# Writing the keys' copy ahead of the values' products over the upper dims, in a four-layer perceiver kernel

## The chip, the cores and the metric

The kernel runs on one core of one Trainium2 chip. The metric is the device time of one execution in microseconds. Before the change the median of 3 runs is 3023.78 us (3019.76 to 3024.86).

## What is computed

A stream `x` of 128 tokens by 256 dims passes four layers. Each layer has a cross-attention over one context of 12544 tokens by 192 dims, an attention among the 128 tokens, and a layer of experts. All of it is float32. What the change touches is the cross-attention of layers 0, 1 and 2, which is in all three of this kind (layer 0 without biases and with a mask over the context, layers 1 and 2 with biases, layer 1 with scores clipped to 10000):

```
q = (layernorm(x) @ Wq + bq)   split in 16 heads of 16
k = (context @ Wk + bk)        split in 16 heads of 16
v = (context @ Wv + bv)        split in 16 heads of 16
out = softmax(q k^T / 4) v
x = x + out @ Wo + bo
```

Layer 3's cross-attention has heads of 64 and code of its own (`KeysInTurn`, `attend_once`).

## The kernel before

**Blocks and groups.** The context is cut in 25 blocks of 512 tokens (`NSB`, `SB`; the last has 256). The 16 heads are two groups `g` of eight, 128 of the 256 dims each. For each group the keys and values of all blocks are made in SBUF, a first sweep over the blocks finds each query's highest score, and a second sweep over chunks of 128 tokens makes exponentials and sums. So a layer has two first sweeps, each of which also projects the keys and values that it will need.

**The context's dims.** A block's context arrives transposed, in two tiles. `ctxA` has the lower 128 dims for 512 tokens. `ctxB` has the upper 64 dims: the first 256 tokens on partitions 0 to 63, the other 256 on partitions 64 to 127. A product over all 192 dims is therefore made in two steps: over `ctxA` (`low` = 0) and, added in PSUM, over `ctxB` (`low` = 1). `halves(b)` lists the two halves of 256 tokens.

**One block's projection** (`project`, L153). The keys and the values of a block share one PSUM tile `p` of 128 partitions by 2 x 512 floats, a "pair". Half `i` holds the keys of its 256 tokens in columns 0 to 255 and the values in columns 256 to 511. `project` is called twice a block. With `low` = 0 it takes a new pair and writes the keys' products over `ctxA` (`keys_into`, L105: two products of 128 x 256) and the values' (`values_into`, L117: four of 128 x 128). With `low` = 1 it adds the same over `ctxB`. Then `keep_keys` (L128) copies the keys to SBUF and `keep_values` (L135) the values; both are one ScalarE instruction (L131 a copy, L133 the same with a bias, L137 a copy). All products are issued by the helper `mm`, L103, so their line is always L103.

**Where blocks are projected.** Each layer projects 44 blocks with values in this way: 8 (layers 1 and 2) or 2 (layer 0) ahead of the attention (`early`, in tiles `kv`, into one PSUM pair of a pool of its own), two between the first group's second sweep and the second group's first (L794), and the rest within the first sweeps. For the last three blocks of a sweep only the keys are made so; their values follow later (`project_values`). Those early blocks and the two between sweeps are placed by the framework's scheduler.

**The order in a first sweep.** `steps` (L139) spreads the blocks to be projected over the 25 steps, two blocks ahead of their use. Within a step `in_order` (L225) keeps TensorE, VectorE and ScalarE to the written order: first the projection, then the scores of the step.

- Masked (layer 0): `highest` is called twice a step. It makes the scores of one block for 8 x 128 queries in two pairs (L558 adds the mask, L559 is the score), and VectorE takes their maxima (L565). Four maxima a step.
- Unmasked (layers 1 and 2): `over` makes scores of the difference of two blocks' keys (L559; the difference is made by GpSimd in `apart`, L570) and ScalarE applies Relu (L578, two a step); `highest_of_two` makes the scores of the other block and VectorE adds them and takes the maximum (L586, four a step).

**PSUM.** In a first sweep the pool `ppr` has four pairs, taken in turn. A step that projects takes five: one for the projection and four for scores. So the last scores of a step take the pair that the projection has just left, and the next projection takes the pair of the step's first scores.

Of the kernel before, what the change touches and what calls it, by code (L numbers as in the profile page):

```python
# [28 lines left out]
HB = SB // 2  # L29
NSB = -(-S2 // SB)  # L30
# [23 lines left out]
class Keys:  # L54
# [98 lines left out]
    def project(self, g, b, low, values=True):  # L153


        if g * NSB + b < self.done:
            return
        if not low:
            self.add_up(g, b)
            self.started[g, b] = self.net.early_pair() if self.rest is None else self.net.pair()  # L160
        p = self.started[g, b]
        self.keys_into(p, g, low, [b])
        if values:
            self.values_into(p, g, low, [b], HB)
        if low:
            n = len(self.halves(b))
            self.keep_keys(g, b, p[:, :n, :HB])
            if values:
                self.keep_values(g, b, p[:, :n, HB:])
            self.done = g * NSB + b + 1  # L170

    def project_values(self, g, blocks):
        p = self.net.pair()
# [1737 lines left out]
```

## Time and profile before

| | |
|---|---|
| median of 3 runs | 3023.78 us |
| the profiled execution | 3021.48 us, span 3019.8 us |
| mean granted TensorE clock | 0.975 |
| L103 into `pair`, keys over ctxA | 1236 products, 399 ns each in the mean |
| L131, keys' copy without bias, 128 x 512 | 586 ns median, 48 + 2 times |
| L133, keys' copy with bias, 128 x 512 | 687 ns median, 100 times |
| L137, values' copy | 579 ns median, 150 times |
| L565, maximum, layer 0 | 1215 ns median |
| L578, Relu, layers 1 and 2 | 1024 ns median |

The first sweeps lie at about 20 to 160 and 280 to 415 us (layer 0), 660 to 760 and 910 to 1030 (layer 1), 1310 to 1430 and 1555 to 1690 (layer 2).

PE is TensorE's products, PEld its loads of the stationary operand, DVE VectorE, ACT ScalarE, POOL GpSimd, SP the queue that issues most DMAs. A line of the timeline gives start, duration, engine, line of the kernel, operation, tile written and tiles read, and how many instructions were merged (`x8`). A float32 product appears as two records. The bracket at the end tells how long the engine was idle before and whose end released it. Ends of products are modelled by the profiler.

### The profile page before, as it was taken

Reading aid. Unit: us, or ns where it says so; the run is one execution under the profiler, and the core shown is the slowest. Engines: PE = TensorE matmul, PEld = TensorE weight load, DVE = VectorE, ACT = ScalarE, POOL = GpSimd, SP = SyncE. Lnnn points to the kernel's source line nnn. Section 1 sums busy time; section 2 is a strip of 40 time slices with the busy share of each in tenths; the row PEclk is TensorE's granted clock in tenths of the full one; section 3 lists DMA queues with packets and bytes.
Section 4 is the critical chain, followed back from the end, with each engine's and each line's share of the span. In section 5 each row is a group of like instructions: output and inputs, shape, how many; then the busy total and the mean of one; then the engine's idle time right before and its main releaser. Section 6 shows DMA issues by size and latency. Waiting matters only on the chain.

```text
span 3019.8 us, 79794 instructions
## 1 busy us (share of the span) xinstructions
PE 2882.8 (95%) x34893; PEld 2209.0 (73%) x34893; DVE 2024.2 (67%) x3241; ACT 1626.2 (54%) x1904; POOL 282.7 (9%) x504
## 2 busy tenths in 40 slices
PE   8999999989999999999999998899999999999969
PEld 5677667455676576765776675688989989889858
DVE  6876887525893598745544555577777777777844
ACT  1176148335685585245875682355655656555521
POOL 7011021223001100211001002000000000000000
PEclk9999999999999999999999998999999999999979
DMA  5201210562002202521012007232322223222436
GB/s 133 61 19 32 72 39 6 189 225 57 21 3 79 59 4 88 175 82 53 15 39 73 23 3 258 92 98 80 85 84 83 85 79 88 85 78 83 136 111 201
DMA packets 177706, 247.28 MB, mean 82 GB/s; under 512 B 32459, under 2 KB 119269, under 8 KB 177358
## 3 DMA queue, kind: packets, MB, share of 16 engines
q1 hardware_dynamic: 165592, 227.26, 24.8%
q0 software_dynamic: 11008, 14.37, 1.6%
q8 instruction: 274, 4.49, 0.6%
q10 hardware_dynamic: 758, 0.55, 0.1%
q14 instruction: 74, 0.61, 0.1%
HBM read 241.56 MB, written 0.13 MB: 80 GB/s over the span
## 4 chain that ended last, share of the span: by engine, by line
PE 83%; DVE 11%; ACT 2%; DMA 1%; issue 1%; SPq 1%; POOL 0%; ACTq 0%; DVEq 0%; POOLq 0%
PE pair L103 21%; PE acc L699 10%; PE pair L559 8%; PE v L103 8%; PE sc L859 6%; PE pair L629 5%; PE acc L901 5%; PE ps L279 5%; PE one L629 4%; DVE parts L565 3%; PE pair L622 2%; PE acc L279 2%; PE kv L103 2%; PE ps L1698 1%; DVE over L586 1%
## 5 line engine op out<-in xcount | busy, mean ns | idle before, releaser
L586 DVE CUSTOM_DVE_ANT_0 over<-over,pair 128x512 f32<-128x512 f32 x384 | 241.2, 683 | 249.2 <-PE pair L559 237.6
L103 PE MATMUL pair<-ctxA,wk 128*128 128x256 f32 x1236 | 328.7, 399 | 6.5 <-ACT over L578 1.8
L103 PEld LDWEIGHTS pair<-ctxA,wk 128*128 128x128 f32 x1236 | 217.0, 190 | 138.5 <-ACT over L578 53.0
L861 ACT COPY kept<-sc 128x1024 f32<-128x1024 f32 (+1 forms) x135 | 136.2, 1009 | 261.2 <-PE sc L859 261.2
L565 DVE TENSOR_REDUCE parts<-pair 128x2 f32<-128x1024 f32 (+1 forms) x216 | 235.7, 1157 | 41.8 <-PE pair L559 41.8
L290 DVE TENSOR_TENSOR top<-top,kept 128x1024 f32<-128x1024 f32 (+2 forms) x145 | 169.1, 1169 | 134.0 <-ACT kept L861 132.7
L293 DVE SCALAR_TENSOR_TENSOR e<-pair,floor 128x1024 f32<-128x1024 f32 x196 | 227.3, 1217 | 14.6 <-PE pair L629 14.6
L677 ACT ACTIVATE e<-pair 128x1024 f32<-128x1024 f32 x196 | 200.7, 1025 | 46.5 <-PE pair L629 26.0
L654 ACT ACTIVATE e<-e 128x1024 f32<-128x1024 f32 x196 | 206.7, 1057 | 35.3 <-DVE e L293 24.3
L629 PE MATMUL pair<-qz,kT 32*128 32x256 f32 x2112 | 218.9, 374 | 0.0
L699 PE MATMUL acc<-e,v 128*17 128x128 f32 x6336 | 211.4, 274 | 3.0 <-ACT e L692 2.2
L699 PEld LDWEIGHTS acc<-e,v 128*17 128x17 f32 x6336 | 155.8, 97 | 67.8 <-ACT e L692 45.6
L692 ACT ACTIVATE e<-e 128x1024 f32<-128x1024 f32 x196 | 205.0, 1048 | 0.0
L293 DVE SCALAR_TENSOR_TENSOR e<-one,maskcol,less 128x256 f32<-128x256 f32 x392 | 162.6, 477 | 53.3 <-PE one L629 43.3
L859 PE MATMUL sc<-qz,kT 64*128 64x128 f32 x2816 | 197.8, 279 | 0.0
L559 PE MATMUL pair<-kT,qz 32*128 32x512 f32 (+1 forms) x1120 | 192.7, 592 | 5.2 <-DVE parts L586 3.8
L578 ACT ACTIVATE over<-pair 128x1024 f32<-128x1024 f32 x192 | 186.9, 1021 | 14.7 <-PE pair L559 7.4
L103 PEld LDWEIGHTS v<-wv,ctxA 128*128 128x128 f32 x1568 | 189.8, 192 | 6.4 <-issue 1.7
L103 PE MATMUL v<-wv,ctxA 128*128 128x128 f32 x1568 | 193.1, 276 | 0.0
L103 PE MATMUL pair<-ctxB,wk 64*128 64x256 f32 x1236 | 188.9, 399 | 0.0
L290 DVE TENSOR_TENSOR e<-one,less 128x512 f32<-128x512 f32 x196 | 126.3, 686 | 88.6 <-PE pair L629 88.1
L859 PEld LDWEIGHTS sc<-qz,kT 64*128 64x128 f32 x2816 | 171.6, 187 | 13.0 <-issue 1.3
(457 smaller groups left out, 5637.7 us busy)
## 6 DMA issues: line engine op xcount, KB each, us to landing
ctxA<-in_ctxA SPq DMA_DIRECT2D x324, 256.0 KB
ctxB<-in_ctxB SPq DMA_DIRECT2D x339, 128.0 KB
w<-in_L_ffn_W SPq DMA_DIRECT2D x32, 1024.0 KB
ctxA<-in_ctxA POOLq DMA_DIRECT2D x36, 256.0 KB, 3.2
w<-in_L_ffn_w_gateT SPq DMA_DIRECT2D x8, 1024.0 KB
wu<-in_L_ffn_w_upT SPq DMA_DIRECT2D x8, 1024.0 KB
w<-in_L_ffn_w_downT SPq DMA_DIRECT2D x8, 1024.0 KB
w<-in_L_ffn_w1T SPq DMA_DIRECT2D x8, 1024.0 KB
```

Of the source, the lines that this page charges most:

```text
L103: self.nc.tensor.matmul(out, a, b, start=start and not low, stop=low == 1, skip_group_check=True)
L279: self.nc.tensor.matmul(out, lhsT, rhs, start=(i == 0), stop=(i == n - 1))
L290: self.nc.vector.tensor_tensor(out, a, b, op)
L293: self.nc.vector.scalar_tensor_tensor(out, a, s, b, op0, op1, **kw)
L559: nc.tensor.matmul(x, qz[r, g, s, :], k[r, :n], start=not by_mask, stop=True)
L565: nc.vector.tensor_reduce(parts[:, s, 2 * half : 2 * half + 2, i], x, AX.X, ALU.max)
L586: nc.vector.tensor_tensor_reduce(es[half][:, j, :], es[half][:, j, :], x[:, j, :], 1.0, -LARGEST, ALU.add, ALU.max, parts[:, s, 2 * half + ...
L629: nc.tensor.matmul(at, keys.kT(c // 4)[tiles[t], k], q, start=start, stop=True, skip_group_check=True)
L654: nc.scalar.activation(to, to, AF.Exp)
L692: nc.scalar.activation(to, to, AF.Exp)
L699: nc.tensor.matmul(acc[32 * t : 32 * t + 17, half, :], v[:, c % 4 + j, 4 * half + t, :], es[half][:, t // 2, j, t % 2, :], start=c + j + h ...
L859: nc.tensor.matmul(x[:, t, c : c + P], kT[r, c : c + P], qz[r, g, :], start=True, stop=True)
```

## The change

In the half with `low` = 1, `keep_keys` now stands between the keys' and the values' products; before it stood behind both. With `low` = 0 nothing differs. `keep_values` and the counter `done` keep their place at the end.

```diff
-        p = self.started[g, b]
+        p, n = self.started[g, b], len(self.halves(b))
+        if not low:
+            self.keys_into(p, g, low, [b])
+            if values:
+                self.values_into(p, g, low, [b], HB)
+            return
         self.keys_into(p, g, low, [b])
+        self.keep_keys(g, b, p[:, :n, :HB])
         if values:
             self.values_into(p, g, low, [b], HB)
-        if low:
-            n = len(self.halves(b))
-            self.keep_keys(g, b, p[:, :n, :HB])
-            if values:
-                self.keep_values(g, b, p[:, :n, HB:])
-            self.done = g * NSB + b + 1
+            self.keep_values(g, b, p[:, :n, HB:])
+        self.done = g * NSB + b + 1
```

## The prediction

> **What bounds the kernel now.** I read the page's engine line first, then the waits, then the timeline of one block in each kind of sweep, because a mean over 3020 us hides which wait ends last in the stage that is changed.
>
> ```profile
> PE 2882.8 (95%) x34893; PEld 2209.0 (73%) x34893; DVE 2024.2 (67%) x3241; ACT 1626.2 (54%) x1904; POOL 282.7 (9%) x504
> PE 83%; DVE 11%; ACT 2%; DMA 1%; issue 1%; SPq 1%; POOL 0%; ACTq 0%; DVEq 0%; POOLq 0%
> ```
>
> TensorE is busy for 95% of the span and makes 83% of the chain that ended last. What stops it inside a block is paid in full, unless it waits a little later anyway. So one block has to be followed. This is a block of layer 0 (the masked kind, four L565 maxima on VectorE):
>
> ```profile
> 77.12 0.73 PEld L103 LDWEIGHTS pair<-ctxA,wk 128*128 128x128 f32 x4 [0.92 <-DVE parts L565]
> 79.08 0.70 PE L103 MATMUL pair<-ctxB,wk 64*128 64x256 f32 x4
> 79.40 0.63 PEld L103 LDWEIGHTS pair<-wv,ctxB 64*128 64x128 f32 x8
> 79.61 0.61 PE L103 MATMUL pair<-wv,ctxB 64*128 64x128 f32 x8
> ...
> 80.27 0.59 ACT L131 COPY kT<-pair 128x512 f32<-128x512 f32 x1 [4.54 <-PE pair L103]
> 80.75 0.59 ACT L137 COPY v<-pair 128x512 f32<-128x512 f32 x1
> ...
> 81.46 4.62 DVE L565 TENSOR_REDUCE parts<-pair 128x2 f32<-128x1024 f32 x4 [1.00 <-PE pair L559]
> 82.74 0.73 PEld L103 LDWEIGHTS pair<-ctxA,wk 128*128 128x128 f32 x4 [0.92 <-DVE parts L565]
> ```
>
> The columns are start, duration, engine, line; the bracket is the idle time before and what ended it. The period is 82.74 - 77.12 = 5.62 us, and it is one closed loop with no slack: 3.03 us of projection on TensorE (77.12 to 80.15, where the next tiles' loads begin), 1.31 us until the first scores are ready (81.46), 1.215 us of the first maximum (median of L565) and a hand-over, whereupon the next projection gets its PSUM pair. The keys' last product ends at 79.08 + 0.70 = 79.78, the values' last at 79.61 + 0.61 = 80.22. The keys' copy starts at 80.27: 0.05 us behind the values, 0.49 us behind the keys.
>
> The same in layer 1 (layer 2 is alike), where the keys' copy adds a bias (L133) and ScalarE also makes the Relu of L578:
>
> ```profile
> 685.06 0.70 PE L103 MATMUL pair<-ctxB,wk 64*128 64x256 f32 x4
> 685.39 0.63 PEld L103 LDWEIGHTS pair<-wv,ctxB 64*128 64x128 f32 x8
> ...
> 686.14 0.31 PEld L559 LDWEIGHTS pair<-apart,qz 32*128 32x128 f32 x8
> 686.26 0.69 ACT L133 ACTIVATE kT<-pair,bk 128x512 f32<-128x512 f32 x1 [2.37 <-PE pair L103]
> 686.84 0.58 ACT L137 COPY v<-pair 128x512 f32<-128x512 f32 x1
> 687.36 1.94 ACT L578 ACTIVATE over<-pair 128x1024 f32<-128x1024 f32 x2
> 688.53 0.73 PEld L103 LDWEIGHTS pair<-ctxA,wk 128*128 128x128 f32 x4 [0.76 <-ACT over L578]
> ```
>
> The period is 688.53 - 683.11 = 5.42 us. Here the two copies stand on ScalarE ahead of the Relu whose end lets the next projection start, so this kind could gain from an earlier copy of the keys. Whether it does is shown by a block that makes keys alone, with no values' copy:
>
> ```profile
> 1020.44 0.31 PEld L559 LDWEIGHTS pair<-apart,qz 32*128 32x128 f32 x8 [0.33 <-issue]
> 1021.67 1.94 ACT L578 ACTIVATE over<-pair 128x1024 f32<-128x1024 f32 x2 [0.42 <-PE pair L559]
> 1022.74 0.73 PEld L103 LDWEIGHTS pair<-ctxA,wk 128*128 128x128 f32 x4 [1.13 <-ACT over L578]
> ```
>
> There ScalarE stands idle for 0.42 us and the Relu still starts 1.23 us behind the load of its products (1020.44), against 1.22 in the full block (686.14 to 687.36). The Relu waits for its products, not for the copies.
>
> **The change, part by part.** *What moves.* In the second half of a block (`low` = 1), one ScalarE instruction moves ahead of four TensorE products. No instruction is added or removed, and no DMA is issued in the moved lines. SP's load into a ctxB buffer waits for the values' products that read it (L397, 80.26), so it comes later by the stall, but it fills the buffer for a block four later, over 20 us. GpSimd's difference of two keys (L570, 1.27 us from 963.53) waits for a block's copies and is needed behind the next projection (964.55 + 3.03), 2.8 us of slack.
>
> *What it adds.* In the built program of the changed kernel the first of the four values' products over the upper dims has a new wait on ScalarE in 131 of 132 blocks, and the values' copy a wait of its own on TensorE. The keys' copy reads columns 0 to 255 of each half of the pair, the products write columns 256 to 511 of the same half; the program orders them as if they overlapped. Before, the order was products, copy; now it is copy, products. TensorE works in order, so behind the waiting product stand the other three, the eight score products of this block, and the next block; VectorE's first maximum (or ScalarE's Relu) waits for those.
>
> *The stall, masked block.* Keys' last product ends at 79.78; +0.05 hand-over as now; +0.586 for the copy (median of L131); +0.05 back to TensorE (the values' copy of 12.24 to 12.83 releases a TensorE load at 12.88) = 80.47, where the values' loads began at 79.40. **1.07 us per block.** A restart costs no more: a projection's keys take 0.76 from the first load to the next tile's both after a wait (77.12 to 77.88) and without one (275.63 to 276.39). Nothing behind gets shorter: the loop from the end of the projection to the next (scores, maximum) does not touch the copies. The two rows that bound this unknown: if the loads go ahead and only the product waits, its start moves from 79.61 to 80.47, 0.86; if the load of 0.21 (79.40 to 79.61) is not hidden at the restart, 1.28. I take 1.07, as every wait of L103 in the timeline holds the load too.
>
> *The stall, biased block.* 685.76 + 0.05 + 0.687 (median of L133) + 0.05 = 686.55 against 685.39: 1.16. ScalarE is free by then: it has been idle since 683.89. One thing comes back: the second copy now ends 0.58 earlier relative to the projection's end, and the last pair of scores, which waits for it, too. In the keys-only block the next projection starts 1022.74 - 1020.44 = 2.30 behind the score loads, in the full block 2.39. So 0.09 is won, since the Relu holds the rest. **1.07 per block**, bounds 0.95 - 0.09 = 0.86 and 1.37.
>
> *How many.* By the values' copies: L137 runs 102 + 30 + 18 = 150 times, 18 of them for values that `project_values` makes apart, so 132 blocks, 44 a layer. 18 lie before the sweeps (the `kv<-kv` copies) and 6 between two sweeps. In the sweeps: 40 masked, 68 biased.
>
> *The sum in the sweeps.* 40 x 1.07 + 68 x 1.07 = 115.6. In two or three of the first masked blocks TensorE waits for other things directly behind (3.17 us ahead of 30.97, for VectorE; 0.67 ahead of 39.95), which covers some 2.5. Left: 113.
>
> *Outside the sweeps* the scheduler, not a written order, places the products. Between the sweeps it sets the next block's 0.75 us of keys ahead of the waiting products, and 9 of 24 weighted products (0.5 us) ahead of the second, which leaves about 0.4 + 0.6 a layer, 3 in all. The 18 early blocks use one PSUM pair: TensorE now waits for both copies behind each (1.25 us, L103 behind L137); it would wait 1.16 in the middle and 0.67 behind, 0.58 more a block. Eight of them lie where weights from DMA end the waits (a wait of 14.70 us for a gate weight is on the chain) and cost nothing; the others have other work set between them. I take 3, from -5 (a lucky order) to 10.4 (18 x 0.58).
>
> *Sum.* 113 + 3 + 3 = 119. The profiled execution took 3021.5 us (span 3019.8): **3140 us**. The median of the runs, 3023.8, is 2.3 above it, less than what is unknown here.
>
> [...]
>
> **The rivals.**
>
> 1. *The stall is covered.* TensorE already idles 0.92 (masked) and 0.76 (biased) ahead of each projection. Were that idle time spent on something the stall does not delay, only 1.07 - 0.92 = 0.15 and 1.16 - 0.76 = 0.40 would be left: 40 x 0.15 + 68 x 0.40 = 33, 3055 us. Against it: both waits end with an instruction that itself waits for scores made behind the stall. 5%.
> 2. *Faster: no wait in effect.* If ScalarE has the keys out before TensorE reaches the values, or the two run side by side, then only the earlier copies count: 0.09 in each of 68 biased blocks, nothing in the masked ones: -6, 3015 us. It decides below a stall of 0.09 us a block; the copy alone takes 0.586. 2%.
> 3. *The clock falls.* The granted clock is 1.00 in the masked sweep and in layer 1's second, with 0.92 and 0.76 of idle loads a block:
>
> ```profile
> 43.00:138.00 95.00, 93.52 (x820) 64.17 (x816) 77.95 (x69) 18.25 (x34) 29.64 (x63) 1.00 0.30 80
> 902.00:1020.00 118.00, 117.45 (x946) 80.69 (x936) 50.35 (x156) 66.07 (x87) 15.10 (x13) 1.00 0.26 74
> ```
>
>    (the column ahead of the last two is the clock). If a second gap of 1.1 us a block lowered it, a projection would cost what layer 2's first does at a low clock, 5.31 us instead of 3.03: 108 x 2.28 = 246 more, 3386 us. 3%.
> 4. *The change does nothing*, should the scheduler put the copy back behind the products: 3022 us. In the sweeps the order is held by hand, and the built program shows the copy's wait moved. 1%.
>
> **How the numbers follow.** The forecast has 89%: 3140 us. Its range: all stalls at 0.86 and the outside at -5: 37.5 masked x 0.86 + 68 x 0.86 - 5 = 86, 3107; all at the upper ends: 40 x 1.28 + 68 x 1.37 + 10.4 + 3 = 158, 3180. So 3106 to 3180; the rivals left out have 11%. Slower by over 0.2%, which is about what a measurement can tell from no change (6 us): forecast, rivals 1 and 3, 97%; same: rival 4 and half of rival 2, 1.5%; faster 1.5%.
>
> **What would show it.** Right: the period in layer 0 is 6.69 and in layers 1 and 2 some 6.49 us; ahead of the values' loads over ctxB stands a wait of about 1 us that the keys' copy (L131, L133) ends; VectorE's idle time ahead of the first maximum grows from 1.00 to about 2.07; the granted clock stays 1.00. Wrong: no wait at L103 on the keys' copy, or a period that keeps 5.62 and 5.42 (rivals 1, 2, 4), projections of over 4.5 us (rival 3), or a Relu that starts clearly sooner than 1.2 us behind its products' loads, which would mean that the copies did hold it.

## The result, and the profile after

The changed kernel takes 3146.24 us (median of 4 runs, 3140.28 to 3152.17) beside 3023.55 us before (4 runs): ratio 1.0408, 95% interval 1.0379 to 1.0437. A second series gave 3143.08 us (4 runs, 3137.43 to 3149.47) beside 3022.11: 1.0403, 1.0384 to 1.0423. It is slower by 121 to 123 us; forecast were 119 and 3140 us. The profiled execution is one of the longer ones, 3152.17 us with a span of 3150.4 and a mean clock of 0.969. In the program's text the added lines move all that stands behind `project` down by two: L559, L565, L578 and L586 are now L561, L567, L580 and L588.

The engines and the chain of the changed kernel:

```profile
PE 2908.9 (92%) x34893; PEld 2201.8 (70%) x34893; DVE 2024.3 (64%) x3241; ACT 1643.9 (52%) x1904; POOL 284.0 (9%) x504
PE 81%; DVE 9%; ACT 6%; issue 1%; DMA 1%; SPq 1%; POOL 0%; ACTq 0%; DVEq 0%; POOLq 0%
```

The counts of instructions are the same, VectorE's busy time too. The span grew by 130.6 us and TensorE's busy time by 26, so TensorE stands still for some 105 us more. ScalarE's share of the chain went from 2% to 6%, by these rounded shares some 130 us more; VectorE's fell from 11% to 9%. The copies now stand on it.

One block of layer 0 in the timeline of the changed kernel:

```profile
80.05 0.70 PE L103 MATMUL pair<-ctxB,wk 64*128 64x256 f32 x4
80.80 0.59 ACT L131 COPY kT<-pair 128x512 f32<-128x512 f32 x1 [4.58 <-PE pair L103]
81.44 0.52 PEld L103 LDWEIGHTS pair<-wv,ctxB 64*128 64x128 f32 x8 [1.09 <-ACT kT L131]
81.44 0.71 PE L103 MATMUL pair<-wv,ctxB 64*128 64x128 f32 x8 [0.69 <-ACT kT L131]
82.08 0.09 PEld L560 LDWEIGHTS <-ones 32*128 32x128 bf16 x1
...
83.39 2.36 DVE L567 TENSOR_REDUCE parts<-pair 128x2 f32<-128x1024 f32 x2 [1.95 <-PE pair L561]
```

The keys' last product ends at 80.05 + 0.70 = 80.75, the copy starts 0.05 behind it and ends at 81.39, and 0.05 later TensorE goes on. The bracket names the copy. Without it the loads would have come 0.32 behind 80.05, at 80.37: a stall of 1.07 us. The next tiles' loads (82.08) then follow 0.64 behind, where it was 0.75 before. The period is 84.67 - 78.10 = 6.57 us, 0.95 more. VectorE stands idle for 1.95 ahead of the first maximum.

One block of layer 1:

```profile
765.42 0.70 PE L103 MATMUL pair<-ctxB,wk 64*128 64x256 f32 x4
766.17 0.69 ACT L133 ACTIVATE kT<-pair,bk 128x512 f32<-128x512 f32 x1 [1.84 <-PE pair L103]
766.91 0.52 PEld L103 LDWEIGHTS pair<-wv,ctxB 64*128 64x128 f32 x8 [1.19 <-ACT kT L133]
767.56 0.31 PEld L561 LDWEIGHTS pair<-apart,qz 32*128 32x128 f32 x8
...
768.78 1.94 ACT L580 ACTIVATE over<-pair 128x1024 f32<-128x1024 f32 x2 [0.52 <-PE pair L561]
...
769.86 0.73 PEld L103 LDWEIGHTS pair<-ctxA,wk 128*128 128x128 f32 x4 [1.13 <-ACT over L580]
```

The stall is 766.91 - (765.42 + 0.33) = 1.16. ScalarE is idle for 0.52 ahead of the Relu, which starts 1.22 behind its products' loads (767.56), as it did before: the earlier copy brought it nothing. The next projection starts 2.30 behind those loads. The period is 769.86 - 763.47 = 6.39 us, 0.97 more.

The clock within the sweeps, from the table of stretches (layer 0's second sweep, layer 1's second):

```profile
308.00:437.00 129.00, 110.75 (x950) 71.11 (x952) 87.79 (x77) 23.45 (x40) 1.12 (x2) 1.00 0.22 61
983.00:1105.00 122.00, 101.29 (x765) 65.98 (x763) 45.38 (x144) 61.29 (x77) 12.01 (x10) 1.00 0.21 61
```

It is 1.00 with the new wait in every block.

**Where the time came from.** From the first to the last projection of each first sweep, in us. For `g` = 1 the stretch begins with the two blocks between the sweeps, which stand directly ahead:

| | L0, g 0 | L0, g 1 | L1, g 0 | L1, g 1 | L2, g 0 | L2, g 1 | all six more | rest of the span more |
|---|---|---|---|---|---|---|---|---|
| before | 130.4 | 129.8 | 100.9 | 124.0 | 101.8 | 123.4 | | |
| after, 3152 us | 152.9 | 149.8 | 118.9 | 144.5 | 115.6 | 144.1 | 115.2 | 15.4 |
| after again, 3137 us | 150.4 | 149.8 | 115.8 | 144.5 | 115.8 | 144.1 | 109.8 | 6.1 |

The three stretches of `g` = 1 are 20.0, 20.5 and 20.6 longer in both executions. The two blocks between the sweeps have 0.8, 1.0 and 0.9 of that. The 20 stalled blocks of each sweep have 19.1, 19.4 and 19.7: 0.96 to 0.99 us a block, as in the single blocks above. The two executions differ in the first sweeps of layers 0 and 1 and in the rest of the span, and their clocks differ too (below).

### The profile page after: what moved, and what is told of

Its sections match the earlier page's. It is cut to its first block, busy times and chain, and to the rows that moved or that the text cites. A ratio compares the mean times of both kernels' runs of the same rounds, so it can differ in the third digit from the quotient of the medians.

```text
span 3150.4 us, 79691 instructions
## 1 busy us (share of the span) xinstructions
PE 2908.9 (92%) x34893; PEld 2201.8 (70%) x34893; DVE 2024.3 (64%) x3241; ACT 1643.9 (52%) x1904; POOL 284.0 (9%) x504
## 4 chain that ended last, share of the span: by engine, by line
PE 81%; DVE 9%; ACT 6%; issue 1%; DMA 1%; SPq 1%; POOL 0%; ACTq 0%; DVEq 0%; POOLq 0%
PE pair L103 21%; PE acc L701 9%; PE v L103 8%; PE sc L861 6%; PE acc L903 6%; PE pair L631 5%; PE pair L561 5%; PE ps L281 4%; PE one L631 4%; DVE parts L567 3%; PE pair L624 2%; PE kv L103 2%; PE acc L281 2%; ACT over L580 2%; PE ps L1700 1%
## 5 line engine op out<-in xcount | busy, mean ns | idle before, releaser
L588 DVE CUSTOM_DVE_ANT_0 over<-over,pair 128x512 f32<-128x512 f32 x384 | 241.3, 684 | 319.3 <-PE pair L561 301.7
L567 DVE TENSOR_REDUCE parts<-pair 128x2 f32<-128x1024 f32 (+1 forms) x216 | 235.9, 1159 | 84.3 <-PE pair L561 84.3
L580 ACT ACTIVATE over<-pair 128x1024 f32<-128x1024 f32 x192 | 186.8, 1021 | 50.9 <-PE pair L561 43.9
L561 PE MATMUL pair<-kT,qz 32*128 32x512 f32 (+1 forms) x1120 | 172.2, 585 | 5.2 <-DVE parts L588 3.8
```

The costliest lines, as they stand in the source:

```text
L561: nc.tensor.matmul(x, qz[r, g, s, :], k[r, :n], start=not by_mask, stop=True)
L567: nc.vector.tensor_reduce(parts[:, s, 2 * half : 2 * half + 2, i], x, AX.X, ALU.max)
L580: nc.scalar.activation(e, x, AF.Relu)
L588: nc.vector.tensor_tensor_reduce(es[half][:, j, :], es[half][:, j, :], x[:, j, :], 1.0, -LARGEST, ALU.add, ALU.max, parts[:, s, 2 * half + ...
```

## The experiments

The theory behind the forecast: TensorE waits in its own order for the keys' copy, because copy and products share a half of a PSUM pair; what that costs is the copy and two hand-overs of 0.05 us, once a block. Rivals were a clock that falls, a restart that costs whatever the copy takes, and the order as such, whatever is read. Each kernel's time stands beside the kernel before in the same series (3021.2 to 3023.4 us). The edits are shown against the changed kernel; only the one that moves the values' copy to VectorE is against the kernel before.

### The changed kernel again

> The changed kernel once more, unaltered, in more rounds. Its four executions so far lie at two levels, 3140.3 and 3152.1 us, 11.8 apart. In the profiled one, at the upper level, the granted clock stays at 0.50 over the first two projections of layer 1's first sweep (703 to 718 us) and over the first of layer 0's (38 to 50), where before it was 1.00 from 663 and from 38. Theory: the two levels are this, the waits that the change adds keep TensorE cold longer at the start of a sweep in some executions: both levels come again, and a profile at the lower level shows a clock of 1.00 within some 6 us of one of these starts or both. Rival: the levels come from elsewhere, and the starts look alike at both.

3143.08 us, between 3137.43 and 3149.47: no two clean levels but a spread of 12 us. The profiled execution was the shortest, span 3135.7, clock 0.974. What the clock withholds, (1 - clock) x span, is 75 us before (0.975), 98 in the execution at 3152 and 82 in this one, each to within 2. The spans of the last two differ by 14.7, the withheld clock by 16. So the spread goes with the clock. The theory of this run said more, that the added waits hold the granted clock at about 0.50 for longer at the starts of sweeps; that is not shown (see the last run). Not all of the spread lies at sweep starts: the first sweeps of layers 0 and 1 have 5.6 of the 14.7, and 5.5 lie between layer 2's last sweep and layer 3's first projections.

### One kind of block at a time

```diff
+        first = self.bias is None
-        self.keep_keys(g, b, p[:, :n, :HB])
+        if first:
+            self.keep_keys(g, b, p[:, :n, :HB])
         if values:
             self.values_into(p, g, low, [b], HB)
+        if not first:
+            self.keep_keys(g, b, p[:, :n, :HB])
+        if values:
             self.keep_values(g, b, p[:, :n, HB:])
```

The other kernel has `is not None` in the first line.

> The keys' copy stands ahead of the values' products in layer 0 alone; layers 1 and 2 have the old order. Theory (TensorE waits out the copy once a block): a period of 6.57 instead of 5.62 us in 40 masked blocks, +38, with some 6 at the cold start of layer 0 and 2 outside the sweeps: 3060 to 3068 us, layers 1 and 2 as before to within 2 us. Rival (the cost comes from another thing that runs on, such as a lower clock, or from where blocks are placed outside the sweeps): far from 3064, or layers 1 and 2 longer too.

> The reverse: the early copy in layers 1 and 2 alone. Theory: 68 blocks by 0.97 = 66, some 6 at layer 1's cold start and up to 9 outside the sweeps: 3092 to 3104 us, layer 0 as before. The excesses of this kernel and of the masked one add up to that of the full change, 117 to 129 us. If they do not add up to within 8 us, the two parts share a cost and the count by blocks is wrong.

The masked one took 3067.81 us (ratio 1.0147, 1.0127 to 1.0166), the biased one 3092.76 (1.0242, 1.0225 to 1.0259). The excesses, 45.7 and 70.7, add up to 116.4, against 121.0 for the whole change in the same series. In the first kernel layer 0's sweeps are 20.0 us longer each and the other four between 0.9 shorter and 1.5 longer; in the second layer 0's are within 0.5 of before and the other four longer by 14.6, 20.5, 13.4 and 20.4. The cost belongs to the blocks, and to within these 5 us it is added up by counting them.

### A shorter and a longer read in the same place

```diff
-        self.keep_keys(g, b, p[:, :n, :HB])
         if values:
+            peek = self.net.stat(2, "peek")
+            self.nc.scalar.copy(peek[:, :n], p[:, :n, 0])
             self.values_into(p, g, low, [b], HB)
+        self.keep_keys(g, b, p[:, :n, :HB])
+        if values:
             self.keep_values(g, b, p[:, :n, HB:])
```

> In the place of the early copy ScalarE makes a copy of 128 x 2 floats out of the keys' columns (some 0.20 us, as its rows of 128 x 8 take), and the keys' copy proper stands behind the values' products as before. One instruction a block is added, in all 132. Theory (the wait is as long as whatever reads the half, and two hand-overs of 0.05): 79.78 + 0.05 + 0.20 + 0.05 = 80.08 against 79.40, 0.68 a block, less the 0.1 that the restart gives back, 0.58: 108 x 0.58 = 63 in the sweeps, 10 to 20 outside: 3092 to 3106 us, and both kinds of period longer by about 0.58. Rival (the wait itself costs, a restart of TensorE or a cold clock, whatever the copy's length): 0.97 a block, about 3145 as with the full copy. Rival (the copy's length is all): 0.2 a block, 3045.

3100.69 us, 1.0262 (1.0247 to 1.0277). The second kernel has `keep_keys` twice in its early place:

```diff
         self.keep_keys(g, b, p[:, :n, :HB])
         if values:
+            self.keep_keys(g, b, p[:, :n, :HB])
             self.values_into(p, g, low, [b], HB)
```

> The changed kernel, with the keys' copy made twice in its early place in all 132 blocks, to the same tile, the second waiting for the first. Three lengths of reading then stand in the same place: 0.16 us in the small read, 0.586 or 0.687 here once and twice. Theory (each further microsecond of reading in that place is a microsecond of the period): 0.59 to 0.64 more a masked block and 0.69 to 0.74 more a biased one: 40 x 0.62 + 68 x 0.72 = 74 in the sweeps and 0 to 15 outside, on 3143 to 3146: 3215 to 3236 us, masked period 7.2, biased 7.1. Rival (part of the wait is slack that a longer read would first fill): under 3205.

3230.23 us, 1.067 (1.0631 to 1.071). The wait in a masked block with the small read, and with two copies:

```profile
89.01 0.70 PE L103 MATMUL pair<-ctxB,wk 64*128 64x256 f32 x4
89.81 0.16 ACT L170 COPY st<-pair 128x2 f32<-128x2 f32 x1 [4.15 <-PE pair L103]
90.02 0.52 PEld L103 LDWEIGHTS pair<-wv,ctxB 64*128 64x128 f32 x8 [0.72 <-ACT st L170]
```

```profile
102.46 0.70 PE L103 MATMUL pair<-ctxB,wk 64*128 64x256 f32 x4
103.21 1.20 ACT L131 COPY kT<-pair 128x512 f32<-128x512 f32 x2 [4.59 <-PE pair L103]
104.46 0.52 PEld L103 LDWEIGHTS pair<-wv,ctxB 64*128 64x128 f32 x8 [1.70 <-ACT kT L131]
```

Reads of 0.16, 0.59 and 1.20 us give idle times of 0.72, 1.09 and 1.70 and periods of 6.20 (83.82 to 90.02), 6.57 and 7.19 (100.51 to 107.70). What is left when the read is taken off is 0.56, 0.50 and 0.50: the end of the keys' last product and the hand-overs. So the price runs with the length of the read, nearly microsecond for microsecond, above a fixed part that even the smallest read pays. This ends the rival in which the wait costs the same whatever is read (3145 expected for the small read), and the one in which a longer read first fills slack.

The clock is another matter with two copies. It (the column ahead of the last two) stays at 1.00 in layer 0's second sweep, but not in layer 1's:

```profile
330.00:450.00 120.00, 94.02 (x800) 60.77 (x804) 77.07 (x67) 29.66 (x51) 0.00 (x0) 1.00 0.21 55
1010.00:1130.00 120.00, 93.49 (x761) 61.38 (x756) 37.67 (x114) 65.76 (x85) 10.19 (x8) 0.97 0.20 57
```

By stretches of 3 us, the clock of layer 1's second sweep falls to 0.79 and 0.64 from 1111 to 1117 us, well inside the sweep, and is 1.00 on both sides. Such falls stand six times in the four biased sweeps of this kernel, away from the low clock at their starts, and never in layer 0's second. Here the period that holds the fall is 8.14 us (1107.49 to 1115.63) and the next is 7.31, where the steady ones are 7.05. The idle time in each biased block is 1.91 us in a period of 7.05 (1100.44 to 1107.49), against 1.70 in 7.19 in layer 0, and the one ahead of this fall is 1.91 too (the loads at 1111.66). In the changed kernel, with 1.19 in 6.39, the biased sweeps show no such fall: by stretches of 3 us the clock is 1.00 beyond their starts. Whether the longer pauses are the cause was not tested.

### Inside and outside the sweeps

```diff
+        first = self.sweeping
```

with `sweeping` set around the projections of a sweep's steps, and the rest as for one kind of block above; the other kernel has `not self.sweeping`.

> The early copy within the six first sweeps alone, 108 of 132 blocks. Theory: the 108 make the cost, about 1.0 each, 110 (from the first to the last projection the six sweeps are 19.96 + 19.95 + 14.9 + 20.45 + 13.9 + 20.6 us longer in the changed kernel): 3126 to 3142 us. Rival (a good part is paid outside, where the scheduler places the products, as the profiled execution at 3152 suggests with 15 us): below 3125.

> The reverse: the early copy in the 18 blocks ahead of the sweeps and the 6 between two sweeps, the old order within. By the prediction's bounds -5 to +13, most likely +6: 3017 to 3035 us, each of the six sweeps as long as before to within 2 us. If it is over 3035, the stages outside hold a cost that was left out.

3127.77 us (1.0351, 1.0331 to 1.037) and 3031.04 us (1.0029, 1.0016 to 1.0042; 12 runs): 104 us (100 to 112) for the 108 blocks in the sweeps, 7.6 (4.8 to 12.7) for the 24 others. The 24 are as the terms of the forecast had them, the 108 are cheaper than its 113. In the first kernel's profile the 20 blocks of the three second sweeps are 19.1, 19.4 and 19.4 us longer, and the two blocks ahead of each are as before: 0.96 us a masked block, 0.97 a biased one. The two excesses add up to 112, 9 less than the whole change cost; with intervals of some 4 to 6 us on each of the three that is not clear of noise.

### Keys and values in pairs of their own

```diff
-            self.started[g, b] = self.net.early_pair() if self.rest is None else self.net.pair()
+            p = self.net.early_pair() if self.rest is None else self.net.pair()
+            self.started[g, b] = p, self.net.pair() if self.rest is not None and values else p
...
-                self.values_into(p, g, low, [b], HB)
+                self.values_into(q, g, low, [b], at)
```

`q` is the second pair and `at` column 0 of it; with one shared pair they are `p` and `HB`. The one kernel copies the keys behind the values' products, the other ahead of them.

> Keys and values of a block get a PSUM pair each (in and between the sweeps; the 18 blocks ahead keep the shared one), the keys' copy stays behind the values' products as before the change. The ring of four pairs is then asked for six a step: the second pair of a projection waits for the previous step's second maximum or Relu, 1.0 to 1.2 us later than the first, where its products come 0.76 us into the projection: 0.3 to 0.5 a block, 108 blocks: 3053 to 3075 us. This is the base for the next kernel.

> The same pairs, with the keys' copy ahead of the values' products over the upper dims as in the changed kernel. Theory (TensorE waits because copy and products share a half of a pair): no wait on the keys' copy is left in the sweeps, so 0 to 12 us more than its base, the 12 from the 18 blocks ahead, which cost 3 to 8 where they were changed alone. Rival (TensorE waits for the copy by its place in the order, whatever it reads): 100 us or more above the base.

3035.26 us (1.0041, 1.0024 to 1.0058; 5 runs) and 3042.51 us (1.0071, 1.0056 to 1.0086). The base is cheaper than expected: the second pair costs about 5.5 us in each of layer 0's sweeps and next to nothing (-0.4 to 1.6) in the others, where I had counted it too. What matters is the difference, 7.3 us where the early copy cost 121 with a shared pair, and as much as the blocks outside the sweeps cost alone; the six stretches of the table differ by 0.9 us in sum between the two kernels. A masked block of the kernel with the early copy:

```profile
88.56 0.70 PE L103 MATMUL pair<-ctxB,wk 64*128 64x256 f32 x4
...
88.88 0.63 PEld L103 LDWEIGHTS pair<-wv,ctxB 64*128 64x128 f32 x8
89.09 0.61 PE L103 MATMUL pair<-wv,ctxB 64*128 64x128 f32 x8
89.31 0.59 ACT L131 COPY kT<-pair 128x512 f32<-128x512 f32 x1 [4.81 <-PE pair L103]
```

The values' loads come 0.32 behind the keys', with no idle time, and the copy (89.31 to 89.90) lies beside the values' products (89.09 to 89.70). Same order, same copy, no wait: the shared pair is the cause. Whether two halves of one pair would wait for each other too, no kernel here tries.

### Other work in the place of the wait

```diff
         self.keep_keys(g, b, p[:, :n, :HB])
+        if between is not None:
+            between()
         if values:
             self.values_into(p, g, low, [b], HB)
```

`between` makes the first call of `highest` (layer 0) or `highest_of_two` (layers 1 and 2) of the step.

> The early keys' copy stays, and the first four scores of the step that do not need this block (the first call of highest in layer 0, highest_of_two in layers 1 and 2) are written between the keys' and the values' products over the upper dims. In layers 1 and 2 the Relu's scores so come behind highest_of_two's. Theory (the cost is TensorE idle behind its own queue, nothing else): four scores take about 1.2 us on TensorE (80.15 to 81.42), more than the copy and two hand-overs, so the wait of 1.07 to 1.16 ahead of the values' products falls under 0.2. What comes instead: the values' copy (0.58) is now late for the last two scores of the step, which take its pair. By hand: the keys' products end at 2.66 in the period, values' at about 4.2, the values' copy at 4.9, the last scores at 5.5 to 6.1: periods of 5.6 to 6.1 instead of 6.57 and 6.39: 3050 to 3105 us. It cannot beat the old order by more than a tenth a block, as TensorE works through 3.03 + 2.50 of the old 5.62. Rival (the wait costs whatever stands behind it, by the clock or the restart): 3137 to 3152 as with the change.

3126.07 us (1.0345, 1.0326 to 1.0364): outside the 3050 to 3105 that I had worked out. A masked block:

```profile
83.81 0.59 ACT L131 COPY kT<-pair 128x512 f32<-128x512 f32 x1 [3.92 <-PE pair L103]
83.92 1.04 PE L563 MATMUL pair<-kT,qz 32*128 32x512 f32 x8
...
84.89 0.72 PE L103 MATMUL pair<-wv,ctxB 64*128 64x128 f32 x8
...
85.66 0.59 ACT L137 COPY v<-pair 128x512 f32<-128x512 f32 x1 [1.26 <-PE pair L103]
85.77 1.02 PE L563 MATMUL pair<-kT,qz 32*128 32x512 f32 x4
...
86.49 1.04 PE L563 MATMUL pair<-kT,qz 32*128 32x512 f32 x4
```

The wait for the keys' copy is gone: TensorE makes eight score products (83.92 to 84.96) while the copy runs, and the values follow at once. But the values' copy now ends at 86.25, and the last scores take its pair. Before, the eight products of a call took 1.04 us together (from 80.38); here four take 1.02 from 85.77 and the other four 1.04, only from 86.49: each four take as long as the eight did. The period is 91.25 - 84.89 = 6.36 us. I had given these last scores half the time that they take. In layers 1 and 2 the sweeps are within 3 us of the changed kernel's. There the Relu's scores now come last, and half of them wait for VectorE:

```profile
1007.54 0.30 PEld L563 LDWEIGHTS pair<-apart,qz 32*128 32x128 f32 x4
1008.47 0.30 PEld L563 LDWEIGHTS pair<-apart,qz 32*128 32x128 f32 x4 [0.63 <-DVE parts L590]
```

The period is 6.45 us (1003.24 to 1009.69), beside 6.39 in the changed kernel. Of the 17 us by which this kernel is faster than the changed one, layer 0's sweeps have 7.7 beside the profile at 3137 us; the rest was not followed, and the clock was higher (0.978). So filling the gap turned one wait into another, in layer 0 one for a copy, and in layer 0 the order of before is the one in which both copies lie beside scores that do not need their pair.

### The values' copy on VectorE, in the old order

```diff
+        if self.sweeping and self.bias is not None:
+            self.nc.vector.tensor_copy(to, p.rearrange("p i (h e) -> p i h e", e=16))
+        else:
+            self.nc.scalar.copy(to, p.rearrange("p i (h e) -> p i h e", e=16))
```

> The old order; in the sweeps of layers 1 and 2 the values' copy is made by VectorE, which stands idle for 2.9 us around it, beside the keys' copy on ScalarE. In the old kernel the last scores of a step wait for the values' copy (0.18 ahead of 687.47) and the next projection starts 2.39 us behind the score loads, against 2.30 where no values' copy stands there. Theory (TensorE's order is at its limit, 3.03 + 2.50 of 5.62 and of 5.42 us, and copies cost only where it waits for them): 0.09 in 68 blocks, -6: 3012 to 3024 us. Rival (copies on ScalarE still hold the Relu): 0.3 or more a block, under 3003. If VectorE is held up by the new copy, over 3027.

3028.48 us (1.0029, 1.0018 to 1.004; 12 runs): a miss, slower where 6 us less were expected. A block of layer 1:

```profile
941.52 0.69 ACT L134 ACTIVATE kv<-pair,bk 128x512 f32<-128x512 f32 x1 [2.62 <-PE pair L104]
...
942.24 0.69 DVE L139 COPY kv<-pair 128x512 f32<-128x512 f32 x1 [1.95 <-ACT kv L134]
...
942.99 0.30 PEld L563 LDWEIGHTS pair<-kv,qz 32*128 32x128 f32 x4 [0.43 <-DVE kv L139]
```

(L139 is the values' copy, L134 the keys'.) VectorE stood idle for 1.95 us and began 0.03 behind the end of ScalarE's copy (942.21), which reads other columns of the same halves. Both copies write `kv` there, in different columns; in the next block they write `kT` and `v`, two tiles, and VectorE again begins 0.03 behind (947.91, behind 947.88), after 1.95 idle. So in these blocks two readers of one half on two engines are taken in turn as well. VectorE's copy is then 0.69 us long, where ScalarE's was 0.58, and the last scores wait 0.43 us for it instead of 0.18: the period went from 5.42 to 5.67 (944.04 to 949.71). The four sweeps are 14.8 us longer together; the span of the profiled execution is only 3.2 longer, at a clock of 0.978, which withholds 9 us less than 0.975. The expectation had "over 3027" for a VectorE that is held up; what came late is the copy, and through it the last scores.

### The kernel before again

> The kernel before, once more, for a second profile. In the one profile so far the granted clock comes back to 1.00 at 38 us in layer 0's first sweep and within 9 us in layer 1's. In the kernels with the early copy in layer 0 it came back at 43 to 53 us, with the old order there at 38 and 36. Theory (the added waits keep the clock low for longer at a cold start): 36 to 38 us again, and about 9 us in layer 1. Rival (the length of the cold phase varies by itself): later than 42 us in layer 0, or over 13 us in layer 1.

One execution, 3015.44 us. The clock is back at 1.00 by 39 to 42 us in layer 0, and in layer 1 by 661, some 10 us after it fell to 0.50. In layer 0 that is a little later than the theory's 36 to 38, and not as late as the rival's 42. The first stretch of 3 us from which layer 0's clock stays at 0.97 or more begins at 36 to 42 us in six kernels with the old order in the sweeps, or the pairs apart and the late copy (before, before_again, biased_only, outside_only, values_on_vector, apart_late), at 45 to 51 in five with a wait (after, again, masked_only, sweeps_only, small_read) and at 48 in fill_early. Yet it is 42 in apart_early, after a second spell at 0.50 (39 to 42 us) and with no wait in its sweep, and 30 in copied_twice, which waits longest. In layer 1, by stretches of 3 us, masked_only with the old order there had a low clock for some 14 us (693 to 707), the changed kernel's second profile for some 10 (695 to 705), about as long as the kernel before in both profiles, and its first for some 17 (703 to 720). That the waits prolong the time at the low clock is therefore not shown. It stays open.

## Why the prediction was right, and where its terms were off

- *The stall.* Right: 1.07 and 1.16 us were forecast for the wait of TensorE, 1.07 and 1.16 are in the timeline, with the hand-overs of 0.05 taken from the old trace. The wait stands where it was looked for, and VectorE's idle time is 1.95 (forecast 2.07).
- *"A restart costs no more."* Off by 0.1 a block, on the good side. After the wait the values' loads need 0.64 us to the next tiles' loads, not 0.75; so the periods are 6.57 and 6.39 us where 6.69 and 6.49 were forecast. The first values' product here starts with its load (81.44 both), where it stood 0.21 behind it before. The row that I had used for a restart was that of the keys' products, which gives 0.76 with and without a wait; it does not carry over to the values'.
- *What comes back in a biased block.* Right: 2.30 us from the score loads to the next projection, 2.39 before, and a Relu 1.22 behind its products' loads.
- *The sum in the sweeps.* Forecast 113. The table's stretches are 110 and 115 longer, but those of `g` = 1 hold the blocks between the sweeps, 2.7 us in all. Without them it is 107 and 112. Of that, 40 x 0.96 + 68 x 0.97 = 104 is the stall of the steady blocks; nearly all of the rest lies in the first sweep of each layer, at whose start the clock is low (0.50 from 36 to 48, 705 to 717 and 1401 to 1404 us in the execution at 3152). So the stall's term, 115.6, was 11 us too large.
- *Outside the sweeps.* Forecast 3 + 3. The change there alone costs 7.6 (4.8 to 12.7), within the bounds given; in its profile the blocks between the sweeps cost 0.8, 1.0 and 0.9 us, 2.7 of the 3 forecast.
- *The clock.* "The granted clock stays 1.00" holds within the steady sweeps, so the rival of 3386 us is refuted. It missed that the low clock varies between executions (it withheld 98 us in the one and 82 in the other, with spans 14.7 apart), which is more than the forecast was off (6 us and 3 us in the two series).
- *Luck in the number.* The forecast came within 6 us although its largest term was 11 us too large. What made up for it are costs that it did not have: low clock at the starts of sweeps, and a part of the rest of the span that was not followed to its lines.
- *The rival of a covered stall.* Refuted for this program, by the idle times of 1.95 on VectorE and 1.13 ahead of the projection, which both grew. Written by hand, a cover hides the wait but leaves 103 us of cost, for reasons that the forecast did not look at: in layer 0 the second copy, in layers 1 and 2 a wait for VectorE.
- *The rival without a wait.* It exists, with a pair for the keys and one for the values: there the early copy costs only what it costs outside the sweeps. But it brings nothing either, since no Relu and no maximum waits for the copies.
- *Two engines at one half.* In the two cases read in the traces the one begins behind the other's end: TensorE's values behind ScalarE's copy (0.05 us, 81.39 to 81.44), and VectorE's copy behind ScalarE's (0.03 us). What happens without the wait was not tried.

No version ran faster than the kernel before: of a masked block's 5.62 us, 3.03 are projection and 2.50 scores, and the two copies lie behind scores.

## What to carry to other kernels

Before moving an eviction earlier, ask which tile TensorE writes next: if it is in the PSUM pair that the eviction reads (here in the same halves of it), the eviction's whole length, the hand-overs and the tail of the last product can stand in TensorE's order; here they did, 1.07 us for a copy of 0.59. The old place behind the last product of the half cost next to nothing here (2.39 us against 2.30 from the score loads to the next projection in a biased block) because the next products went to another pair. And VectorE, idle for 1.95 us, was of no help to a half that ScalarE was reading: its copy began only 0.03 us behind the end of ScalarE's.

## What the runs showed of the hardware that was not expected

- Behind a wait of 1.09 us the first of eight 64x128 products starts together with its load, and the next tiles' loads follow 0.64 us behind. Without a wait the loads begin 0.21 ahead of the products, beside the keys' last ones, and the next loads follow 0.75 behind. The products themselves are not faster behind the wait (0.71 us against 0.61).
- The same program's span varied between 3135.7 and 3150.4 us at mean clocks of 0.974 and 0.969; the clock fell to 0.50 for some 3 to 17 us at the starts of sweeps, and for how long was not the same in two executions of one kernel. Layer 0's start in the execution at 3152 us, with the clock in the column ahead of the last two:

```profile
45.00:48.00 3.00, 2.31 (x13) 1.44 (x12) 0.00 (x0) 0.59 (x1) 3.00 (x7) 0.50 0.61 175
48.00:51.00 3.00, 3.00 (x23) 1.54 (x24) 0.47 (x1) 0.59 (x1) 2.67 (x7) 0.51 0.31 55
51.00:54.00 3.00, 3.00 (x22) 1.97 (x18) 3.00 (x4) 0.00 (x0) 3.00 (x7) 1.00 0.08 9
```

  In the execution at 3137 us it was 1.00 from 45 us. In layer 1 the execution at 3152 us had 0.50 from 703 to 718 us, the one at 3137 us 0.64 from 703 to 706 and 1.00 from 706. What sets the length was not shown.
- With idle times of 1.09 and 1.19 us ahead of the values' loads in every block the clock was 1.00 over 129 us of layer 0's second sweep and 122 us of layer 1's, and so it was with 1.70 in the masked blocks with two copies (over 120 us). With 1.91 in 7.05 us, in the biased blocks with two copies, it fell six times in four sweeps (to 0.79 and 0.64 in two stretches of 3 us, 1111 to 1117 us). So the rival of a falling clock, refuted for this change, is not refuted for longer pauses; whether they make it fall was not tested.
